# A four-layer convolution network: layer 2's patches stored as lines by column offsets by channels, and the product instructions that read them

## The chip, the core and the metric

The kernel runs on one core of a Trainium2 chip. The metric is the device time of one execution in microseconds (us); the median of the runs of the kernel before is 8996.71 us. The engines are named as the profile names them: PE (TensorE) multiplies matrices, PEld loads its weights, DVE is VectorE, ACT is ScalarE, POOL is GpSimd, and SP is the queue from which this kernel issues its DMAs. SBUF is the on-chip memory of 128 partitions; PSUM is the memory that TensorE writes.

## The reference: what is computed

The input is 16 images of 64 x 64 positions with 256 channels, all float32. Four layers follow one another, each of the form `x = x + layer(groupnorm(x))`. The change concerns layer 2 alone, an involution: a small network makes nine weights for each position and each of 16 groups of channels, and these weigh the 3 x 3 patch of a projected image.

```
r = relu(norm(x @ Wr + br))                         # 64 channels
w = (r @ Ws + bs).reshape(B, H, W, G, KK)[:, :, :, :, None, :]
xi = x @ Wi + bi
xp = pad(xi)                                        # one position on each side
patches = stack([xp[:, i:i+H, j:j+W, :] for i in range(3) for j in range(3)], axis=3)
patches = patches.reshape(B, H, W, G, F // G, KK)
out = sum(w * patches, axis=-1)                     # 256 channels
```

The reshape is what makes the order of numbers matter. Before it, a position's 2304 numbers are ordered by tap (three lines by three columns) and then by channel. After it, the same 2304 numbers are cut in order into 256 outputs of nine numbers each. So output channel o takes the numbers 9 o to 9 o + 8 of the run. These nine are nine neighbouring channels of one tap, or, where the run passes from one tap to the next, the last channels of one and the first ones of the other. Sixteen neighbouring outputs share a group, and so the nine weights.

## The kernel before

**Stages.** The kernel runs through four stages with pools of their own: layer 0 and the gates of layer 1, then layer 1's scan, then a stage in which the end of layer 1, all of layer 2 and the preparation of layer 3 overlap, and at last layer 3. Only the third stage holds the change. In the profile its products run from 3865 to 6521 us.

**Turns.** The third stage is a loop over turns with an order of instructions written out by hand (`tc.manual_schedule()`). Each image has NCH = 8 turns, and a turn takes four lines of the upper half of an image together with four lines of the lower half; a column position and a half make up the 128 partitions (`(w g)`, w the 64 columns, g the half). Four jobs run in each turn, each for another image, offset by `LAG = (0, 12, 20, 30)` turns: the end of layer 1 (`end_of_layer1`), the projection Wi (`projected`), the involution, and the centring of the finished output for layer 3 (`centred`). A job drops out where its images have ended, so that the involution runs in 128 turns, the first 10 of them without centring and the last 20 or so without the end of layer 1.

**What a turn issues, in order.**
- SP: the loads for the next turn (`loads`, L964: x2p and x2r, which are layer 2's input for the projection and for the weights; x1 and pf for the end of layer 1), the stores of the turn before (L1241: x2, x3, c3, and 16 `strips` stores for centred lines), then the load of xc for the next turn's centring. xc has two buffers, so its load waits until the strips of two turns before have been read. x2p has two buffers too, so its load waits for the projection (L1061) that read the older one.
- TensorE: the later half's weights (`weights`, L1092); the preparation of the next turn, which is the reduction Wr (`reduced2`, L1082), the patches' transposes (L1108) and the first half's weights; the residual's transposes (`residual`, L1128, tile lo); the finished turn's transposes (`turned`, L1162); the projection (L1061).
- ScalarE: the preparation's activation (L1085) and the patch copies out of PSUM (L1112) with the copies at the seams (L1114, L1118), all in `patches`; then the activation on z (L1004) of the end of layer 1, the copies of the finished turn (L1163), the projection's activation into the padded lines (L1065), and squares for the statistics (L1183, L1015).
- GpSimd: two additions of the end of layer 1 (L1008), which need ScalarE's z; then the sums of the first half (`sums_on_pool`: three additions L1149 and one L1150), then the subtraction of the mean in `centred` (L900).
- VectorE: two instructions of the end of layer 1 (L998, tiles z and pf), the products of the first half and of the second half (`products`, L1138), the sum of the second half over nine (a reduction, L1284), and two additions of the residual (L1287), the second of which needs GpSimd's L1150.

When the next turn is the first of an image, its preparation is put behind the first half's products, because the padded lines are only complete then. The norms between the layers are chains of small instructions that are advanced one piece at each `step()`.

**Patches.** `patches` makes for each turn three tiles xs, one for each column offset j (pool `b_xs`, six buffers). A tile holds six lines (four and one more on each side) of 256 channels, and eight more numbers at the end of each line. These eight are the first channels of the next offset (L1114) or, behind the third offset, those of the next line (L1118), so that nine numbers that pass a seam can be read from one tile.

**Products.** `involution_segments` cuts the 256 outputs wherever a tap begins and wherever a group of 16 begins. That gives 24 segments, each with its tap, its first channel, its first output and its count n. For each segment one instruction multiplies four lines by n outputs by nine numbers with the group's nine weights, which lie in PSUM (pw) and are read again for each of the n outputs. The result goes to the tile pd, [128, 4, 128, 9] for a half of 128 outputs. Twelve segments belong to each half. Eight segments of the 24 have all 16 outputs of a group, 576 numbers in each partition; the others have 36 to 540. Together they are 9216 numbers in each partition and turn.

Of the kernel before, what the change touches and what calls it, by code (L numbers as in the profile page):

```python
# [9 lines left out]
F32 = mybir.dt.float32  # L10
# [5 lines left out]
P = 128  # L16
C = 256
# [13 lines left out]
TILE_IN = (TR + 6) * (TC + 6)  # L31
TILE_OUT = TR * TC
SPAN = P + (TR - 1) * (TC + 6) + TC - 1


def involution_segments():

    cuts = sorted({-(-tap * C // 9) for tap in range(10)} | set(range(0, C + 1, 16)))  # L40
    return [(9 * o // C, 9 * o % C, o, n - o) for o, n in zip(cuts, cuts[1:])]


@with_exitstack
def network(ctx: ExitStack, tc: tile.TileContext, a: dict, out: bass.AP):
    nc = tc.nc
# [138 lines left out]
    with ExitStack() as st:  # L185
# [399 lines left out]
        for n in range(LAST + 16):  # L585
            m, t = divmod(n, NCH)
# [26 lines left out]
            def between(dp):  # L613
                step()
                if dp == 0:
                    for p in parts:
                        if p is not parts[0]:
                            next(p)
                    for p in parts:
                        next(p, None)  # L620
                    for p in old:
                        next(p, None)
                    for p in projecting:
                        next(p)
# [26 lines left out]
    with ExitStack() as st:  # L651
# [24 lines left out]
        with tc.tile_pool(name="s_conv", bufs=1) as pcv:  # L676
# [20 lines left out]
            for delta in range(-2, 3):  # L697
                for rr in range(2):
                    for r2 in range(2):
                        di = 2 * delta + rr - r2 + 3  # L700
# [8 lines left out]
        for n in range(10):  # L709
            delta, c = n // 2, n % 2  # L710
# [28 lines left out]
        with tc.manual_schedule():  # L739
# [25 lines left out]
            for n, (ch, g) in enumerate(steps):  # L765
# [18 lines left out]
                b, k = g * 8, min(8, NI - g * 8)  # L784
# [8 lines left out]
        n = NI * NCH  # L793
        pt = tr.tile([P, CT], F32, tag="tr", name="pt")
# [125 lines left out]
    with ExitStack() as st:  # L920
        pc = st.enter_context(tc.tile_pool(name="b_const", bufs=1))
        wk = st.enter_context(tc.tile_pool(name="b_work", bufs=2))
        xs_p = st.enter_context(tc.tile_pool(name="b_xs", bufs=6))
        pd_p = st.enter_context(tc.tile_pool(name="b_pd", bufs=2))
        tr = st.enter_context(tc.tile_pool(name="b_tr", bufs=3, space=PSUM))
        pwp = st.enter_context(tc.tile_pool(name="b_pw", bufs=3, space=PSUM))
# [23 lines left out]
        for b in range(2):  # L950
# [2 lines left out]
            nc.vector.memset(rt[64:65, :], 1.0)  # L953
            rts.append(rt)

        segments = involution_segments()
        st0, st3, gn2, ngm2 = {}, {}, {}, {}
        loaded, stores, begun = [], [], []

# [138 lines left out]
        def patches(i, rc, between):  # L1098


            xs = []
            for j in range(3):
                t = xs_p.tile([P, 6, C + 8], F32, tag="xs", name="xs")
                for e in range(0, 6, 2):
                    pt = tr.tile([P, 2, C], F32, tag="tr", name="pt")
                    for k in range(2):
                        for h in range(2):
                            nc.tensor.transpose(  # L1108
                                pt[:, k, h * P : (h + 1) * P],
                                lines[:, h, rc * 4 + e + k, 2 * j : 2 * j + P], ident,  # L1110
                            )
                    nc.scalar.copy(t[:, e : e + 2, 0:C], pt)  # L1112
                if j:
                    nc.scalar.copy(xs[-1][:, :, C:], t[:, :, 0:8])  # L1114
                xs.append(t)
                if j == 0:
                    between()
            nc.scalar.copy(xs[2][:, 0:5, C:], xs[0][:, 1:6, 0:8])  # L1118
            return xs

        def residual(x2):
# [8 lines left out]

        def products(oh, pw, xs):
            pd = pd_p.tile([P, 4, P, 9], F32, tag="pd", name="pd")
            for tap, c0, o, n in segments:
                if o // P != oh:
                    continue
                di, dj = tap // 3, tap % 3
                w0 = o // 16 * 9 - oh * 72
                nc.vector.tensor_tensor(  # L1138
                    pd[:, :, o - oh * P : o - oh * P + n, :],
                    xs[dj][:, di : di + 4, c0 : c0 + 9 * n].rearrange("p r (f k) -> p r f k", k=9),  # L1140
                    pw[:, :, w0 : w0 + 9].unsqueeze(2).broadcast_to([P, 4, n, 9]),
                    ALU.mult,
                )
            return pd
# [87 lines left out]
        with tc.manual_schedule():  # L1232
            loads(0)
            ahead, made = None, None
            for n in range(TURNS):
# [21 lines left out]
                def prepare():  # L1257
                    x2r, rt = reduced2(*nxt)
                    ahead = [x2r, rt]
                    ahead.append(patches(*nxt, lambda: ahead.append(weights(rt, 0))))  # L1260
                    return ahead
# [11 lines left out]
                if inv:  # L1273
                    pd = products(0, now[2], now[3])
                    sums_on_pool(pd, x3)
                if nxt and not nxt[1]:
                    ahead = prepare()
                if inv:
                    pd1 = products(1, w1, now[3])
# [19 lines left out]
    with ExitStack() as st:  # L1299
# [201 lines left out]
        for n, (i, quarter, t) in enumerate(turns):  # L1501
# [45 lines left out]
            if n in features:  # L1547
                tp, k = features[n]
# [118 lines left out]
```

## Time and profile before

| what | value |
|---|---|
| runs shown | 8993.86, 8996.71, 9007.82 us |
| span of the profiled execution, first to last instruction | 8940.3 us |
| median less span, what lies around it | 56.4 us |
| mean granted TensorE clock | 0.913 |
| stretch 4112 to 5249 us (1137 us): VectorE busy | 1080 us |
| the same stretch: TensorE, ScalarE, GpSimd busy | 858, 714, 802 us |
| the same stretch: DMA engines busy, bytes moved | 0.82, 223 GB/s |
| the same stretch: granted TensorE clock | 0.85 |

No time is listed beside the profiled execution but its span, so what lies around that span is taken from the median of the runs. In the page's list of costliest groups a line reads: source line, engine, operation, output and inputs by name with partitions x elements, the count, then after the first bar the busy time of the group in us and the mean of one instruction in ns, and after the second bar the idle time of the engine just before these instructions and what ended most of it. Busy time counts a moment once even where two instructions of an engine overlap, so it can be less than count by mean. In the list of waits a line reads: engine and line that waited, what it waited for, the total in us, how often, and the longest. In the timeline a line reads: start and length in us, engine, line, operation and operands, the number of instructions merged, and in brackets the idle time before it with what ended it; SPq is the issuing of DMAs. In the slices each digit stands for 223.5 us.

### The profile page before, as it was taken

To read this page: it belongs to the slowest core of one execution; us is meant where nothing else is said; L and a number is where in the kernel's file an instruction comes from. 1 tells how busy PE (TensorE), PEld (TensorE's weight loads), DVE (VectorE), ACT (ScalarE), POOL (GpSimd) and SP (SyncE) were. 2 spreads that over 40 slices of the span, in tenths; PEclk is the share of its full clock that TensorE was granted. 3 is DMA by queue.
4 is the path that set the end of the run, shared out by engine and by line. 5 is a ranking of instruction groups with operands and counts; after the bars stand their busy time and mean duration, and the time that the engine had idled before them with its cause. 6 is when DMAs were issued, how large, how long until landed. Compare 5 with 4: busy or idle time off the path is not lost. (4 is left out here: it accounts for less than half of the span.)

```text
span 8940.3 us, 213550 instructions
## 1 busy us (share of the span) xinstructions
PE 7239.3 (81%) x84764; PEld 5334.1 (60%) x84764; DVE 6515.6 (73%) x10687; ACT 5059.9 (57%) x12288; POOL 2767.6 (31%) x1962
## 2 busy tenths in 40 slices
PE   7988889888899977477777777777758888888888
PEld 4666666666666653145545444455546666777776
DVE  6676666676666665679999999999945555566665
ACT  3555555555555554666666666665535555566665
POOL 0111111111111110156776776776621111111122
PEclk9999999999999986888888888888879999999999
DMA  6533333333333333767888888887768787888887
GB/s 220 167 121 123 125 123 122 124 123 120 125 109 105 108 110 110 257 205 209 220 225 225 221 227 220 221 230 208 186 165 256 243 252 240 254 258 260 267 260 244
DMA packets 1617992, 1695.63 MB, mean 190 GB/s; under 512 B 855265, under 2 KB 1221170, under 8 KB 1615842
## 3 DMA queue, kind: packets, MB, share of 16 engines
q1 hardware_dynamic: 1616994, 1681.98, 62.1%
q8 instruction: 668, 10.94, 0.5%
q14 instruction: 330, 2.70, 0.1%
HBM read 1234.54 MB, written 469.76 MB: 191 GB/s over the span
## 5 line engine op out<-in xcount | busy, mean ns | idle before, releaser
L287 PE MATMUL pq<-wq,xn 128*128 128x384 f32 x4096 | 1471.9, 503 | 105.3 <-DVE va L303 57.5
L1138 DVE TENSOR_TENSOR pd<-xs,pw 128x576 f32<-128x576 f32 (+15 forms) x3072 | 1438.2, 554 | 10.0 <-PE pw L1092 6.6
L1403 ACT ACTIVATE wm<-pk,spanb 128x176 f32<-128x176 f32 x2560 | 988.6, 543 | 520.8 <-PE pk L1393 500.4
L1408 DVE TENSOR_TENSOR wm<-pk,spanb 128x704 f32<-128x704 f32 x896 | 1174.5, 1354 | 142.5 <-PE pk L1393 130.2
L1393 PE MATMUL pk<-rt,span 64*128 64x176 f32 x12288 | 1199.2, 331 | 96.3 <-issue 44.3
L1149 POOL TENSOR_TENSOR pd<-pd 128x2048 f32<-128x2048 f32 (+2 forms) x384 | 1065.4, 2775 | 296.3 <-DVE pd L1138 276.3
L287 PEld LDWEIGHTS pq<-wq,xn 128*128 128x128 f32 x4096 | 762.7, 195 | 573.8 <-DVE va L303 90.9
L1393 PEld LDWEIGHTS pk<-rt,span 64*128 64x128 f32 x12288 | 982.0, 193 | 196.6 <-issue 67.7
L1477 POOL TENSOR_TENSOR ex<-ex,rx 128x192 f32<-128x192 f32 (+2 forms) x768 | 435.4, 570 | 1855.5 <-DVE ex L1470 1211.0
L1459 PE MATMUL pa<-wm,xw 126*32 126x48 f32 x45056 | 701.4, 211 | 237.2 <-issue 198.3
L1470 DVE SCALAR_TENSOR_TENSOR ex<-pa,msk,ex 128x192 f32<-128x192 f32 x704 | 292.1, 415 | 745.9 <-ACT ex L1469 717.5
L1459 PEld LDWEIGHTS pa<-wm,xw 126*32 126x32 f32 x45056 | 578.1, 112 | 410.7 <-issue 341.1
L1061 PE MATMUL px<-x2p,wis 128*128 128x512 f32 x1024 | 581.4, 711 | 139.6 <-ACT c L1163 99.5
L1108 PEld LDWEIGHTS pt<-ident,pad 128*128 128x128 f32 x4608 | 542.1, 151 | 252.5 <-issue 78.0
L1108 PE MATMUL pt<-ident,pad 128*128 128x128 f32 x4608 | 628.2, 292 | 74.4 <-ACT rt L1085 43.3
L1112 ACT COPY xs<-pt 128x512 f32<-128x512 f32 x1152 | 604.1, 588 | 139.6 <-PE pt L1108 137.4
L456 POOL TENSOR_TENSOR rsy<-ss,mhalf 128x4 f32<-128x4 f32 x128 | 129.8, 1014 | 1704.2 <-DVE ss L454 1704.2
L1284 DVE TENSOR_REDUCE x<-pd 128x512 f32<-128x4608 f32 x128 | 634.1, 4954 | 1.9
L444 PE MATMUL py<-wo,oT 128*128 128x256 f32 x2048 | 472.5, 383 | 28.9 <-DVE va L303 28.9
L1469 ACT ACTIVATE ex<-pa,msk 128x192 f32<-128x192 f32 x704 | 297.6, 423 | 330.7 <-PE pa L1459 229.2
L1082 PE MATMUL pr<-x2r,wrs 128*64 128x512 f32 x512 | 317.7, 754 | 198.3 <-DMA x2r<-x_d 185.2
L303 DVE COPY va<-pq 128x256 f32<-128x256 f32 x512 | 216.6, 423 | 336.2 <-ACT ka L299 315.3
(240 smaller groups left out, 12764.3 us busy)
## 6 DMA issues: line engine op xcount, KB each, us to landing
xw<-strips SPq DMA_DIRECT2D x1408, 256.0 KB
xn<-in_x SPq DMA_DIRECT2D x256, 512.0 KB
x_d<-x SPq DMA_DIRECT2D x256, 512.0 KB
strips<-xc SPq DMA_DIRECT2D x1536, 56.0 KB
xin<-in_x SPq DMA_DIRECT2D x128, 512.0 KB
x<-in_x SPq DMA_DIRECT2D x128, 512.0 KB
xm<-x_d SPq DMA_DIRECT2D x128, 512.0 KB
x<-x_d SPq DMA_DIRECT2D x128, 512.0 KB
```

The lines of the kernel that those rows point to most:

```text
L287: nc.tensor.matmul(pq[:, dd, 0:384], lhsT=xn[:, h, tok], rhs=wq[:, h, hf * 384 : (hf + 1) * 384], start=(h == 0), stop=(h == 1),)
L444: nc.tensor.matmul(py[:, q, :], lhsT=oT[hf][:, q * P : (q + 1) * P], rhs=wo[:, hf, :], start=(hf == 0), stop=(hf == 1),)
L1061: nc.tensor.matmul(px, lhsT=w[:, h, fh * P : (fh + 1) * P], rhs=x2[:, h], start=(h == 0), stop=(h == 1),)
L1108: nc.tensor.transpose(pt[:, k, h * P : (h + 1) * P], lines[:, h, rc * 4 + e + k, 2 * j : 2 * j + P], ident,)
L1112: nc.scalar.copy(t[:, e : e + 2, 0:C], pt)
L1138: nc.vector.tensor_tensor(pd[:, :, o - oh * P : o - oh * P + n, :], xs[dj][:, di : di + 4, c0 : c0 + 9 * n].rearrange("p r (f k) -> p r f ...
L1149: nc.gpsimd.tensor_tensor(pd[..., 0:n], pd[..., 0:n], pd[..., n : 2 * n], ALU.add)
L1284: nc.vector.tensor_reduce(x3[:, :, P:C], pd1, AX.X, ALU.add)
L1393: nc.tensor.matmul(pkv[:, b, m], lhsT=span[half, first + gg, s0 : s0 + P], rhs=rto[half, o // 4 * 2 + m, :], start=True, stop=True,)
L1403: nc.scalar.activation(dst[:, m // 2, m % 2], pkv[:, m // 2, m % 2], AF.Identity, bias=spanb[:, g0 + m : g0 + m + 1],)
L1408: nc.vector.tensor_tensor(dst, pkv, spanb[:, g0 : g0 + 4].rearrange("p (b m) -> p b m", b=2).unsqueeze(3).broadcast_to([P, 2, 2, NTL]), AL ...
L1459: nc.tensor.matmul(pav[p0 : p0 + 32, :, tj * TC : (tj + 1) * TC], lhsT=xw[0:TILE_IN, k, tj, 32 * q : 32 * q + 32], rhs=wm[q][0:TILE_IN, (t ...
```

## The change

The three tiles of a turn become one block, six lines by three column offsets by 256 channels, with two buffers. In it a line's three offsets lie one behind the other, and the next line follows at once; so the 2304 numbers of an output line (three lines by three offsets by 256 channels) are one run in memory. The eight extra numbers per line and the copies at the seams (L1114 and L1118 before) go, and `involution_segments` goes with them. The products are cut by line and half: an instruction takes one of four output lines and one half, 1152 numbers of the run as eight groups by 16 outputs by nine numbers, with the line's weights in PSUM read for each of the 16 outputs. That is 8 instructions a turn, where there were 24. The tile pd, the sums, the transposes and the nine patch copies (two lines of 256 channels each) keep their shapes; a patch copy now writes its two lines 768 numbers apart and not 264.

```diff
-def involution_segments():
-    cuts = sorted({-(-tap * C // 9) for tap in range(10)} | set(range(0, C + 1, 16)))
-    return [(9 * o // C, 9 * o % C, o, n - o) for o, n in zip(cuts, cuts[1:])]
...
-        xs_p = st.enter_context(tc.tile_pool(name="b_xs", bufs=6))
+        xs_p = st.enter_context(tc.tile_pool(name="b_xs", bufs=2))
...
-            xs = []
+            xs = xs_p.tile([P, 6, 3, C], F32, tag="xs", name="xs")
             for j in range(3):
-                t = xs_p.tile([P, 6, C + 8], F32, tag="xs", name="xs")
                 for e in range(0, 6, 2):
...
-                    nc.scalar.copy(t[:, e : e + 2, 0:C], pt)
-                if j:
-                    nc.scalar.copy(xs[-1][:, :, C:], t[:, :, 0:8])
-                xs.append(t)
+                    nc.scalar.copy(xs[:, e : e + 2, j, :], pt)
                 if j == 0:
                     between()
-            nc.scalar.copy(xs[2][:, 0:5, C:], xs[0][:, 1:6, 0:8])
             return xs
...
             pd = pd_p.tile([P, 4, P, 9], F32, tag="pd", name="pd")
-            for tap, c0, o, n in segments:
-                if o // P != oh:
-                    continue
-                di, dj = tap // 3, tap % 3
-                w0 = o // 16 * 9 - oh * 72
+            for r in range(4):
+                run = xs[:, r : r + 3].rearrange("p e j c -> p (e j c)")
                 nc.vector.tensor_tensor(
-                    pd[:, :, o - oh * P : o - oh * P + n, :],
-                    xs[dj][:, di : di + 4, c0 : c0 + 9 * n].rearrange("p r (f k) -> p r f k", k=9),
-                    pw[:, :, w0 : w0 + 9].unsqueeze(2).broadcast_to([P, 4, n, 9]),
+                    pd[:, r].rearrange("p (g f) k -> p g f k", f=16),
+                    run[:, oh * 9 * P : (oh + 1) * 9 * P].rearrange(
+                        "p (g f k) -> p g f k", f=16, k=9
+                    ),
+                    pw[:, r].rearrange("p (g k) -> p g k", k=9).unsqueeze(2).broadcast_to(
+                        [P, 8, 16, 9]
+                    ),
                     ALU.mult,
                 )
             return pd
```

More of the change, by code (lines that the diff above doesn't have):

```diff
@@ L954, in network @@
             rts.append(rt)
-        segments = involution_segments()
         st0, st3, gn2, ngm2 = {}, {}, {}, {}
```

## The prediction

> **What bounds the kernel now.** The products run in one stage, layer 2, from 3865 to 6521 us. I read first the page's slices and costliest groups, to see which engine is full there.
>
> ```profile
> DVE  6676666676666665679999999999945555566665
> ...
> POOL 0111111111111110156776776776621111111122
> ...
> DMA  6533333333333333767888888887768787888887
> ...
> L1138 DVE TENSOR_TENSOR pd<-xs,pw 128x576 f32<-128x576 f32 (+15 forms) x3072 | 1438.2, 554 | 10.0 <-PE pw L1092 6.6
> ...
> L1284 DVE TENSOR_REDUCE x<-pd 128x512 f32<-128x4608 f32 x128 | 634.1, 4954 | 1.9
> ```
>
> VectorE is at nine tenths and the products are more than half of it, but the DMA engines are at eight tenths and move only 223 GB/s. A full engine need not set the pace, so I read who the DMA queue (SP) waits for, first in 3850 to 4100 us, then in 5200 to 6130 us, then in 6530 to 6600 us:
>
> ```profile
> SPq L964 <- PE px L1061: 146.5, 12, 17.3
> ```
> ```profile
> SPq L964 <- DMA strips<-xc: 78.7, 90, 2.1
> ...
> SPq L964 <- PE px L1061: 3.7, 8, 0.7
> ```
> ```profile
> SPq L1309 <- PE pv L156: 15.5, 1, 15.5
> ```
>
> At first SP waits for compute in each turn (a load needs the buffer that projected, L1061, has not yet read). In the middle it waits for nothing but DMAs. At the very end it waits 15.5 us for compute, before the first load of layer 3. Now the timeline: the loads of x2r mark SP's turns, the products VectorE's.
>
> ```profile
> 5331.19 0.43 SPq L964 DMA_DIRECT2D x2r<-x_d  x1
> ...
> 5353.83 0.43 SPq L964 DMA_DIRECT2D x2r<-x_d  x1
> ...
> 5375.68 0.43 SPq L964 DMA_DIRECT2D x2r<-x_d  x1
> ```
> ```profile
> 5343.67 11.23 DVE L1138 TENSOR_TENSOR pd<-xs,pw 128x576 f32<-128x576 f32 x24
> 5354.94 4.95 DVE L1284 TENSOR_REDUCE x<-pd 128x512 f32<-128x4608 f32 x1
> 5360.00 1.34 DVE L1287 TENSOR_TENSOR x<-x,lo 128x512 f32<-128x512 f32 x2
> 5361.83 1.64 DVE L998 SCALAR_TENSOR_TENSOR z<-x,ngm,pf 128x512 f32<-128x512 f32 x1 [0.49 <-DMA pf<-fac_d]
> 5363.51 0.75 DVE L998 SCALAR_TENSOR_TENSOR pf<-x,ngm,pf 128x512 f32<-128x512 f32 x1
> ```
>
> I listed all 128 x2r loads and reductions (number i: the i-th of each) and took differences:
> - Head, i = 0 to 12 (to 4112 us): reductions 18.9 to 20 us apart, but for i = 1 (25.9) and two turns after an image's end (24.5 and 22.6). VectorE sets the pace.
> - Middle, to i = 108 (6175 us): SP's turns stay at 20.6 to 22.6 us, mean 21.58 from i = 9 to 65 and 21.6 from 65 to 105. VectorE needs 20.0 to 20.5, and 25 to 30 once per image. It starts behind and closes up: reduction i comes 69.7 us after load i at i = 9, 47.5 at 65, then never under 42.6. From there it takes SP's pace, and TensorE waits for SP:
>
> ```profile
> PE pr L1082 <- DMA x2r<-x_d: 115.6, 28, 7.8
> ```
> - Tail, i = 108 to 127: layer 1's loads have ended. SP's turn is 18.0, VectorE's 17.5 and without a gap (11.23 products, 4.95 reduction, 1.28 additions). VectorE sets the pace.
>
> [...] Trace: 24 products of 9216 elements take 11.23 us, so (11.23 - 9.60 - 0.09)/24 = 64 ns each, the 0.09 being the last one's own tail[...]. [...] z (L998) takes 0.75 us alone, and 1.64 above while GpSimd's subtraction runs (L900, to 5362.92); products always take 11.23 for 24. [...]
>
> **The change part by part.** Groups by form in 4500 to 6500 us:
>
> ```profile
> L1138 DVE TENSOR_TENSOR pd<-xs,pw 128x576 f32<-128x576 f32 x768 | 578.6, 753 | 4.9 <-PE pw L1092 4.9
> ...
> L1138 DVE TENSOR_TENSOR pd<-xs,pw 128x288 f32<-128x288 f32 x192 | 78.9, 457 | 0.0
> ...
> L1114 ACT COPY xs<-xs 128x48 f32<-128x48 f32 x192 | 44.5, 232 | 6.1
> ...
> L1118 ACT COPY xs<-xs 128x40 f32<-128x40 f32 x96 | 21.1, 220 | 0.0
> L1138 DVE TENSOR_TENSOR pd<-xs,pw 128x36 f32<-128x36 f32 x96 | 18.5, 192 | 0.0
> ```
>
> 1. Products. From 36 to 576 elements the time grows 561 ns for 540, 1.04 ns each[...]. So 8 instructions of 1152 need 8 x 1.20 + 8 x 0.064 + 0.09 = 10.20 us, not 11.23: 1.03 less a turn, half in each half. One should show 1152/0.96 + 154 = 1.35 us (154 is what 753 has over 576/0.96). Inner runs stay 9 long; outer steps change, and no row has this form. Bounds: all fixed cost gone, -1.54 us; a tenth slower streaming, back to nothing. I take 1.03.
> 2. The copies at seams: 2 x 232 + 220 = 0.68 us of ScalarE a turn. They lie ahead of z's activation (L1004), GpSimd's additions (L1008) and its sums (L1149) in ScalarE's and GpSimd's order. Hidden by VectorE in most turns of head and tail; on the path after an image's end, where VectorE waits 4.45 us at 4048 us for the sums, two preparations being in that chain (1.37 us).
> 3. Patch copies (L1112) stay nine of 512 elements, 588 ns, with a longer step between two lines: taken at nothing, as VectorE's turn covers it; +-20 ns each would be +-0.18 us where ScalarE isn't covered.
> 4. Buffers: one block per turn twice, not three tiles six times, equally two turns deep. A block is free when the later half's last product is done, a turn before it is written: nothing (were that order to fail, a patch copy would wait for products, up to 10.2 us). The products' waits, for pw and for the copies, are those of before, and no DMA, matrix or GpSimd instruction moves: their order is unchanged.
> 5. New wait? GpSimd's sums and last addition take 8.45 + 1.65 = 10.1 us from the end of the first products; VectorE reaches its addition after 5.1 + 4.98 + 0.65 = 10.7 (11.2 before). 0.6 us to spare, so none of its own.
>
> Where it counts:
> - Head: i = 0 about 0.7 (half of products, or copies), 1 to 6 six full turns 6.2, the image's end 1.4, i = 9 1.0, then 0.5 each for two turns in which z now stands longer before GpSimd's subtraction. 10 us, handed to SP, which waits there for compute.
> - Middle: SP's turn of 21.6 stays. VectorE (about 19.2) only catches up sooner. Once locked, the way from x2r's landing to the reduction loses 0.68 + 1.03, a single gain of about 2.
> - Tail: 19 turns x 1.03 = 19.6, less about 0.6 at the image's end: 19.
> Sum 31. Against it: x2r lands about 7.5 us after issue (TensorE waits for it at 6395.87 for 6388.37), then 3.6 projection, 0.8, 7 patches, 10.2 products = 29 us least lag; the last lag of 48.4 would fall to 27, so 2 come back. And SP's 15.5 us rest before layer 3, in which its transfers drain, goes: about 3. SP itself ends 10 earlier, plus 5 that it waits for GpSimd's subtractions (L900) in the tail, so it can follow. Result 31 - 2 - 3 = 26 us.
>
> The profiled span is 8940.3 us, the median of the runs 8996.7; the 56 between lie outside the span. I take 26 off both: 8914 and 8971.
>
> **The rivals.**
> - A: SP sets the pace of the tail too (its turn of 18.0 is over VectorE's 17.5 already, with few waits for compute). Then only the head counts: 10 us, 8987. For it: 24 transfers a turn, 16 of them strips of 10.5 us in all. Against: the lag grows from 37.9 to 48.4 in the tail, and the 15.5 us wait at its end. Chance 0.20.
> - B: VectorE sets the pace throughout, and SP only looks free: 128 x 1.03 = 132 us, 8865. For: 0.95 busy. Against: VectorE closing up on SP by 22 us in the middle. Chance 0.07.
> - C, slower: [...] From 10.7% slower on (1.03 of 9.6) the turn grows. At 25% it is 2.40 - 1.03 = 1.37 more a turn, over 10 + 19 turns of head and tail 40; in the middle 20.3 + 1.4 is just over SP's 21.6, and the 25 to 30 once per image is no longer made up, some 5 for each of 12 images, 60 more: 9097. For: untried pattern. Against: 36 to 576 elements on one line. Chance 0.07.
> - D: it doesn't do what it says, the fixed cost being tied to something other than the count: 8997, chance 0.05.
>
> **How the numbers follow.** The forecast has 0.61, with its own range 8961 to 8982. A measurement of this kernel can tell about 0.2%, 18 us: faster means under 8979, slower over 9015. The forecast gives 0.53 faster and 0.08 same, A 0.20 same, B 0.07 faster, D 0.05 same, C 0.07 slower; that is 0.60, 0.33 and 0.07. The range takes in A: 8955 to 8993; B, C and most of D lie outside, under 0.2.
>
> **What would show it.** Products near 1.35 us each and 10.2 for 8; no seam copies; SP's turns 21.6 in the middle as before; first strips issued about 10 us earlier; reductions 16.5 apart in the tail; the lag falling sooner and ending near 29; the wait ahead of layer 3's first load mostly gone. It is wrong if the middle's turns shorten (B), if the tail's reductions stay 17.5 or TensorE waits for x2r in each of its turns (A), or if a product takes over 1.5 us (C).

## The result and the profile after

The kernel after takes 8967.52 us (median of five runs, 8952.84 to 8976.86), the kernel before 8996.71 us (8991.18 to 9008.92) on the same chip. That is 29 us less, a ratio of 0.9963 with a 95% interval of 0.9951 to 0.9975.

The execution profiled after has a span of 8974.9 us and took 8976.86 us. So 2 us lie around a span, not the 56 that stood between the first profile and its median. Two further profiles of the kernel before show the same 2 us: spans of 8937.8 and 8949.0 us for times of 8939.59 and 8950.74. The first profile, with a span of 8940.3 us, therefore belongs to an execution of about 8942 us, some 50 us faster than every run listed beside it. That it came from another chip is an estimate, from the 8946.59 us that the kernel before takes on the chip of e1 to e4; the record does not show it. So the spans of the two first profiles are not subtracted from one another, and the time is followed piece by piece on one chip below. Lengths of instructions and kinds of waits are still read side by side.

From the page of the kernel after, three slices and VectorE's two rows of the involution:

```profile
DVE  6676666776666665679989988999946565566665
...
POOL 0111111111111110157766666676712121111112
...
DMA  6533333333333333867878878887768888888887
...
L1121 DVE TENSOR_TENSOR pd<-xs,pw 128x1152 f32<-128x1152 f32 x1024 | 1305.6, 1349 | 13.3 <-ACT xs L1102 13.3
...
L1271 DVE TENSOR_REDUCE x<-pd 128x512 f32<-128x4608 f32 x128 | 633.7, 4951 | 1.9
```

VectorE has lost some of its nines in the middle, while the DMA digits stay. The products cost 133 us less (1438.2 before), while the run is 29 us shorter. The waits of SP, in the windows of the prediction (3850 to 4100, 5200 to 6130, and the last stretch before layer 3, 6480 to 6600 us):

```profile
SPq L955 <- PE px L1052: 132.4, 13, 15.7
```
```profile
SPq L955 <- DMA strips<-xc: 79.2, 94, 2.5
...
SPq L955 <- PE px L1052: 8.2, 13, 1.1
```
```profile
SPq L1296 <- PE pv L148: 2.1, 1, 2.1
```

SP waits less for compute in the head (132.4 us for 146.5), still for hardly anything but DMAs in the middle, and 2.1 us instead of 15.5 ahead of layer 3's first load. SP's timeline and VectorE's in the middle:

```profile
5344.20 0.43 SPq L955 DMA_DIRECT2D x2r<-x_d  x1
...
5366.03 0.43 SPq L955 DMA_DIRECT2D x2r<-x_d  x1
...
5387.13 0.43 SPq L955 DMA_DIRECT2D x2r<-x_d  x1
```
```profile
5355.91 10.20 DVE L1121 TENSOR_TENSOR pd<-xs,pw 128x1152 f32<-128x1152 f32 x8
5366.14 4.95 DVE L1271 TENSOR_REDUCE x<-pd 128x512 f32<-128x4608 f32 x1
5371.20 0.69 DVE L1274 TENSOR_TENSOR x<-x,lo 128x512 f32<-128x512 f32 x1
5373.01 0.69 DVE L1274 TENSOR_TENSOR x<-x,lo 128x512 f32<-128x512 f32 x1 [1.12 <-POOL x L1137]
5374.23 1.61 DVE L989 SCALAR_TENSOR_TENSOR z<-x,ngm,pf 128x512 f32<-128x512 f32 x1 [0.53 <-DMA pf<-fac_d]
```

SP's turns are 21.8 and 21.1 us, as long as before. The products have fallen to 10.20 us, and VectorE now waits between its two additions and ahead of z. TensorE's wait for x2r in 5200 to 6130 us was 122.1 us before and is now

```profile
PE pr L1073 <- DMA x2r<-x_d: 163.5, 31, 8.3
```

Much of what VectorE saves in the middle (1.03 us in each of this window's 43 turns, 44 us) returns as waiting for SP's loads (41 us more). Groups by form, 4500 to 6500 us:

```profile
L1121 DVE TENSOR_TENSOR pd<-xs,pw 128x1152 f32<-128x1152 f32 x768 | 979.2, 1349 | 9.4 <-ACT xs L1102 9.4
...
L1102 ACT COPY xs<-pt 128x512 f32<-128x512 f32 x864 | 444.0, 602 | 92.4 <-PE pt L1098 90.2 <-DVE z L989 0.3 <-DVE pd L1121 0.2
```

The seam copies are gone; a patch copy is recorded with 602 ns, where it had 588.

### The profile page after: what moved, and what is told of

It reads as the page before. It is cut to its first block, busy times and chain, and to the rows that moved or that the text cites. A ratio compares the mean times of both kernels' runs of the same rounds, so it can differ in the third digit from the quotient of the medians.

```text
span 8974.9 us, 210876 instructions
## 1 busy us (share of the span) xinstructions
PE 7219.9 (80%) x84764; PEld 5328.9 (59%) x84764; DVE 6420.8 (72%) x8639; ACT 4992.0 (56%) x11904; POOL 2764.1 (31%) x1962
## 5 line engine op out<-in xcount | busy, mean ns | idle before, releaser
L1121 DVE TENSOR_TENSOR pd<-xs,pw 128x1152 f32<-128x1152 f32 x1024 | 1305.6, 1349 | 13.3 <-ACT xs L1102 13.3
L1380 PE MATMUL pk<-rt,span 64*128 64x176 f32 x12288 | 1217.4, 334 | 108.5 <-issue 58.5
L1073 PE MATMUL pr<-x2r,wrs 128*64 128x512 f32 x512 | 364.5, 853 | 374.3 <-DMA x2r<-x_d 368.5
L1052 PE MATMUL px<-x2p,wis 128*128 128x512 f32 x1024 | 531.7, 664 | 111.4 <-ACT c L1150 68.2
L445 ACT ACTIVATE sq<-y 128x256 f32<-128x256 f32 x512 | 213.0, 416 | 422.6 <-DVE y L441 414.6
```

The lines of the kernel that those rows point to most:

```text
L1052: nc.tensor.matmul(px, lhsT=w[:, h, fh * P : (fh + 1) * P], rhs=x2[:, h], start=(h == 0), stop=(h == 1),)
L1121: nc.vector.tensor_tensor(pd[:, r].rearrange("p (g f) k -> p g f k", f=16), run[:, oh * 9 * P : (oh + 1) * 9 * P].rearrange("p (g f k) -> ...
L1380: nc.tensor.matmul(pkv[:, b, m], lhsT=span[half, first + gg, s0 : s0 + P], rhs=rto[half, o // 4 * 2 + m, :], start=True, stop=True,)
```

## The experiments

The theory is the prediction's: SP sets the pace in the middle, VectorE in head and tail. The rivals are A (SP in the tail too) and B (VectorE throughout). Each run is compared with the kernel before on its own chip: 8946.59 us for e1 to e4, 8985.80 for e5 to e8, 8956.67 for e9 to e12. "Stage" is the time from the first reduction of layer 2 to the first product of layer 3 in the profile (tile pk); it leaves out what an execution happens to lose elsewhere. The expectations were written with the first chip's 8996.71 us in mind, so what counts in them is the distance to the kernel before or after.

| run | time, us | ratio to before, interval | stage, us |
|---|---|---|---|
| e1 before | 8939.59 (single run) | | 2730.4 |
| e2 after, third xc buffer | 8829.66 | 0.9874 (0.9861 to 0.9888) | 2617.5 |
| e3 before, third xc buffer | 8916.83 | 0.9970 (0.9958 to 0.9981) | 2688.4 |
| e4 after, 32 products in the middle | 8918.63 | 0.9972 (0.9963 to 0.9982) | 2704.1 |
| e5 after | 8942.21 | 0.9952 (0.9938 to 0.9966) | 2716.2 |
| e6 after, 64 products in the head | 8972.64 | 0.9988 (0.9981 to 0.9994) | 2749.0 |
| e7 after, 64 products in the tail | 9007.94 | 1.0029 (1.0018 to 1.0039) | 2785.1 |
| e8 after, one more load a turn | 9057.47 | 1.0083 (1.0069 to 1.0097) | 2838.2 |
| e9 before | 8950.74 (single run) | | 2734.8 |
| e10 after | 8927.70 (single run) | | 2709.7 |
| e11 e2 with seam copies | 8898.94 | 0.9932 (0.9920 to 0.9944) | 2686.8 |
| e12 e2 with a late subtraction | 8988.90 | 1.0032 (1.0020 to 1.0045) | 2769.4 |

**e1, e5, e9, e10: the two kernels again**, without an edit.

> The kernel before, unchanged, profiled a second time, to set the two profiles side by side from the same day's chip. The first profile of before spans 8940 us while its runs take 8991 to 9009; the profile of after spans 8975 while its runs take 8953 to 8977. Theory (SP sets the pace in the middle of layer 2, and the rest is chance of the execution): the products' stage, from the first reduction to the last, takes 2643 us as in the first profile (within 8), and layer 3 takes anything between 2328 and 2375. Rival (the change itself made layer 3 some 40 us longer): layer 3 takes 2328 again, within 5.

> After, unchanged, timed beside before on one chip, so that the edits can be set against it. On the chip of the first experiments before took 8946.6. Both theories: 29 us under before, within 8; profile: products' stage from first to last reduction 14 us shorter than in before, as in the first profile of after, or 25 if the middle's slower SP turns there were chance of that execution.

> Before, unchanged, profiled beside after on the same chip, since the profiles so far came from chips of different speed. Theory (SP's turn in the middle is the chip's, not the form's): from load 14 to load 105 both take the same within 5 us; from the first reduction to the first load of layer 3, after is 20 to 28 us shorter; layer 3 is equal within 8. Rival (the faster form itself lengthens SP's turn, by 0.1 us a turn): the middle is 8 us or more longer in after.

> After, unchanged, profiled beside before on the same chip; the numbers are those said for before.

On the second chip the change is worth 44 us, which is 7 more than e5's expectation allowed (29 within 8); its interval, 31 to 56 us, overlaps that of the first chip, 22 to 44. The single runs on the third differ by 23. e1 does not decide its question: layer 3 takes 2331.6 us, which the theory (2328 to 2375) and the rival (within 5 of 2328) both allow. The profiles of e9 and e10 decide it, and let the time be followed piece by piece (the i-th x2r load and the i-th reduction of 128, counted from 0, as in the prediction):

| piece | e9 before | e10 after | difference |
|---|---|---|---|
| first instruction to first reduction | 3878.2 | 3882.5 | +4.3 |
| head: first reduction to x2r load 14 | 228.0 | 214.2 | -13.8 |
| middle: x2r load 14 to 108 | 2027.6 | 2026.2 | -1.4 |
| lag: load 108 to reduction 108 | 43.6 | 41.3 | -2.3 |
| tail: reduction 108 to 127 | 344.7 | 337.1 | -7.6 |
| last reduction to first product of layer 3 | 90.9 | 90.9 | 0.0 |
| layer 3 | 2336.0 | 2333.5 | -2.5 |

The stage is 25 us shorter. SP's turn in the middle is 21.57 us before and 21.56 after, and layer 3 differs by 2.5 us, so both rivals fall: the new form lengthens neither.

**e4: the middle's products in 32 instructions of 288 numbers.** Turns 30 to 99 only; k is the number of the turn, and g0 runs over the eight groups of a line and half.

```diff
+            m = 2 if 30 <= k < 100 else 8
...
-                nc.vector.tensor_tensor(
-                    pd[:, r].rearrange("p (g f) k -> p g f k", f=16),
...
+                for g0 in range(0, 8, m):
+                    o = (oh * 8 + g0) * 144
+                    nc.vector.tensor_tensor(
+                        pd[:, r, g0 * 16 : (g0 + m) * 16].rearrange("p (g f) k -> p g f k", f=16),
...
```

> After, with the products of the middle alone (turns 30 to 99 of the 128) cut into 32 instructions of 288 numbers, not 8 of 1152: 24 x 0.064 = 1.54 us more VectorE a turn. SP theory: VectorE's turn of 19.2 becomes 20.7, still under SP's 21.7, so nothing but slack goes: 8968 to 8985. Rival VectorE: 70 x 1.54 = 108 more, 9075.

It is 28 us faster than the kernel before (12 to 29 were expected), within the 23 to 44 of the kernel after, though its middle's turns hold 24 instructions more. The first of the two waits, 4550 to 6140 us, is of e4, the second of the kernel after:

```profile
PE pr L1073 <- DMA x2r<-x_d: 234.7, 51, 7.1
```
```profile
PE pr L1073 <- DMA x2r<-x_d: 281.9, 54, 8.7
```

Of the 108 us that the products add (70 turns by 1.54), 47 are seen here as less waiting of TensorE for x2r (in the same window e9, the kernel before, has 159.2 us and e10, the kernel after, 277.1); the rest was not followed. SP's turn is 21.54 us, 21.52 in e1 on the same chip. Rival B, by which this kernel had to be some 80 us slower than the kernel before, falls.

**e6: the head's products in 64 instructions of 144 numbers**, e4's edit with `m = 1 if 0 <= k < 12 else 8`.

> After, with the products of the first 12 turns alone cut into 64 instructions of 144 numbers: 56 x 0.064 = 3.6 us more VectorE in each of these turns. SP theory: in the head SP waits for compute, so 12 x 3.6 = 43 us are handed to it and are never made up: 35 to 45 us over after. Rival (slack of the middle absorbs a late head, as the distance between SP and VectorE falls from 60 to 43 anyway): under 20 us over after.

It takes 30 us more than e5. The timeline of e6 shows a turn of the head:

```profile
3919.97 4.95 DVE L1272 TENSOR_REDUCE x<-pd 128x512 f32<-128x4608 f32 x1
3925.03 1.28 DVE L1275 TENSOR_TENSOR x<-x,lo 128x512 f32<-128x512 f32 x2
3926.24 0.74 DVE L989 SCALAR_TENSOR_TENSOR z<-x,ngm,pf 128x512 f32<-128x512 f32 x1
3927.02 0.75 DVE L989 SCALAR_TENSOR_TENSOR pf<-x,ngm,pf 128x512 f32<-128x512 f32 x1
3927.68 13.81 DVE L1124 TENSOR_TENSOR pd<-xs,pw 128x144 f32<-128x144 f32 x64
```

The products take 13.81 us, 3.61 more than 10.20, and VectorE has no gap. x2r load 14 leaves 243.2 us after the first reduction, 213.7 in e5. These 29.5 us stay to the end: the head hands what it loses to SP, and the rival (under 20) falls. The forecast of 35 to 45 was too high, since not every turn loses 3.6 us: from one reduction to the next turns 2 to 8 lose 3.6, but turn 1 only 0.7 and turn 9, at the image's end, 0.9, and turn 12 gains 1.0 back.

**e7: the tail's products in 64 instructions**, e4's edit with `m = 1 if 108 <= k < 128 else 8`.

> After, with the products of the last 20 turns alone cut into 64 instructions: 3.6 us more VectorE in each, a turn of 20.1 against SP's 18.0. Theory (VectorE sets the pace of the tail and the entry into layer 3 waits for it): 20 x 3.6 = 72, less the slack of SP's end, which is at most a few us: 60 to 72 us over after. Rival A (SP sets the pace of the tail too): only what exceeds SP's 18.0, 20 x 2.1 = 42 or less.

It takes 66 us more than e5. Of 20 turns by 3.61 = 72, nine tenths arrive. The wait of SP ahead of layer 3 is back:

```profile
SPq L1297 <- PE pv L148: 19.3, 1, 19.3
```

SP is done and waits, so VectorE is what the tail ends with. Rival A falls.

**e8: one more load a turn.** In turns 35 to 124 x2p is loaded a second time, into a tile that nothing reads. To have room, two tiles of layer 0 and 1 (`maps`, `fac`) move to a pool that is closed ahead of the stage; e2, e3, e11 and e12 do so too.

```diff
+            if proj and 35 <= n < 125:
+                t = wk.tile([P, 2, CT], F32, tag="x2q", name="x2q", bufs=1)
+                nc.sync.dma_start(out=t, in_=x2_d[proj[0], proj[1]])
```

> After, with one more load of 512 KB a turn (x2p a second time into a tile that nobody reads) in 90 turns of the middle, no work for any engine changed. SP theory: at 223 GB/s, 512 KB are 2.3 us of SP's turn, so 90 x (1.5 to 2.3) = 135 to 210 us over after. Rival VectorE: nothing, within 10.

It takes 115 us more than e5, 1.28 us for each of 90 loads; SP's turn goes from 21.63 to 22.90 us. The price, 135 to 210, was put too high, but a transfer that gives no engine any work goes into the time, where B had nothing. TensorE's wait for x2r, 4550 to 6140 us, in e8:

```profile
PE pr L1076 <- DMA x2r<-x_d: 358.9, 58, 11.9
```

**e2 and e3: a third xc buffer**, after and before. The strips and the load behind them no longer wait for the strips of two turns ago.

```diff
-            ))
+            ), bufs=3)
```

> After, with a third buffer for xc, so that its load need not wait for the strips of two turns before to land (4 KB more for each partition, found by giving two tiles that are dead by then a pool of their own). SP theory: SP waits 1.9 us a turn for this in the middle (138 us in 155 waits from 4550 to 6140 us); its turn falls from 21.7 to about 19.8, VectorE's own turn (19.2, and once per image more, 20.2 in the mean) then decides, and 94 turns x 1.4 = 130 us go: 8835, from 8800 to 8900. Rival VectorE (it sets the pace already): within 10 of 8968. Rival DMA throughput (the engines, not the queue's order, are full): the wait comes back as longer issues, SP's turn stays above 21.2, 8930 to 8968.

> Before, with the same third buffer for xc. SP theory: VectorE's own pace in the middle is 21.2 in the mean, SP's 21.6, so 95 x 0.4 = 38 us go: 8958, from 8930 to 8975; and the product change is then worth 8958 - 8835 = 120 us, four times what it is worth with two buffers. Rival VectorE: 8997, and the difference between the two forms stays at 29. Rival DMA throughput: 8960 to 8997, difference still about 29.

With SP's wait gone, e3 is 30 us faster than the kernel before and e2 117: where SP no longer sets the pace, the change is worth 87 us instead of 23 to 44. SP's turn in the middle falls to 20.59 us in e2 (21.52 in e1), with the same transfers, so the rival that the DMA engines themselves are full falls too. SP's waits in e2, 4300 to 6000 us, show that it now waits for compute, the DMA that headed the list being gone from its top:

```profile
SPq L958 <- PE px L1055: 69.9, 19, 6.4
SPq L1231 <- POOL xc L894: 57.2, 31, 4.8
SPq L1231 <- DMA x_d<-x: 56.8, 118, 2.1
```

This is the fastest kernel, 1.26% under the kernel before. But 87 is not the 120 expected, and z is why in part: its mean in this window is 1476 ns in e2 and 1202 in e3. In the first profiles of the two kernels (3860 to 6180 us) a z that meets no subtraction of GpSimd's takes 0.74 to 0.76 us (64 and 69 of them), and each one that meets one (L900 before, L892 after) ends 0.54 to 0.62 us behind it (44 and 40), whether it began early or late in it. So a VectorE that comes sooner makes z longer. A second part is one turn of each image, three after the one that follows an image's end: from one reduction to the next it takes 22.6 us in e2 and 20.5 in e3 (mean of turns 30 to 104).

**e11: e2 with the seam copies alone put back.** They write a tile that nothing reads.

```diff
+            seam = wk.tile([P, 6, 8], F32, tag="seam", name="seam", bufs=2)
...
+                if j:
+                    nc.scalar.copy(seam, xs[:, :, j, 0:8])
...
+            nc.scalar.copy(seam[:, 0:5, :], xs[:, 1:6, 0, 0:8])
```

> After with the third buffer for xc, and with the three copies at the seams put back on ScalarE (into a tile that nobody reads), the products as in after. This splits the 87 us that the change is worth with the third buffer (8916.8 to 8829.7 on one chip) into its two parts. Theory (the copies only count in the chain after an image's end, two preparations each): 15 images x 1.4 = 21 us over the third buffer alone, so 96 us under before instead of 117. Rival (the copies lie ahead of GpSimd's sums in each turn): 60 us or more of the 87. Rival (all is the count of instructions): within 5.

Of the 117 us against the kernel before 58 are left, so the copies cost 59 of the change's 87; by the stages (own chip's before taken off) it is 65 of 71. The 21 us expected were far too few, and the rival that only the count of instructions matters falls. The other rival has nearly the right size (60 or more), but not the place, as it had the copies count in each turn. The wait of VectorE for GpSimd's sums and of GpSimd for z's activation, 4300 to 6000 us, in e2 and then in e11:

```profile
DVE x L1277 <- POOL x L1140: 66.8, 20, 5.5
```
```profile
POOL x L1002 <- ACT z L998: 208.0, 62, 10.0
```
```profile
DVE x L1281 <- POOL x L1144: 121.5, 20, 9.1
```
```profile
POOL x L1002 <- ACT z L998: 314.2, 60, 13.6
```

As many turns, 20, wait nearly twice as long in all. Mean turns by place in the image (turns 30 to 104) tell where (from one reduction to the next): e2 has 24.7 us in the turn after an image's end and 22.6 three turns later, e11 29.1 and 24.0; the other six differ by 0.1 at most. 5.8 us an image hang on copies of 0.68 us, two preparations of which (1.37) lie in that chain. Why it is four times their own length was not found. That it lies in the chain ScalarE, GpSimd, VectorE is shown by the two waits.

e11 set against e3 leaves the count of instructions, 8 for 24, since both have copies at the seams and the third buffer (e11's copies write another tile, and the chips differ). It is worth 28 us by the times and only 6 by the stages. In the middle it brings nothing: x2r load 14 to 108 takes 1996.0 us in e11 and 1980.1 in e3, and the two chips differ there by only 5 (2027.6 and 2022.9 for the kernel before). Six turns of each image are about 0.5 us shorter, but the two in which VectorE waits for GpSimd's sums are longer, 29.1 and 24.0 us for 27.5 and 20.5.

**e12: the subtraction of the centring a turn later**, with a fourth xc buffer, so that z should be free of it.

```diff
+                if late:
+                    centred(*late)
                 if inv:
...
-                if cen:
-                    centred(*cen)
+                late = cen
```

> After with a fourth buffer for xc and GpSimd's subtraction of the mean (2.37 us) moved from the end of a turn into the next turn, behind the two additions and ahead of the sums, where GpSimd waits 2.4 us for products anyway. With the third buffer alone z on VectorE takes 1.46 us in the mean, not 0.75[...]; theory: VectorE's turn loses 0.7 to 1.2 us in some 90 turns, but SP's issues alone are near 19 us a turn, so 40 us (20 to 70) are gained over the third buffer alone: 137 to 187 us under before. Rival (SP and the DMA engines now decide): within 15 of the third buffer alone, 102 to 132 under before.

The time went the other way: it is 32 us slower than the kernel before. z did what was hoped, the sums did not, 4300 to 6000 us of e12:

```profile
L992 DVE SCALAR_TENSOR_TENSOR z<-x,ngm,pf 128x512 f32<-128x512 f32 x77 | 57.6, 748 | 1.6 <-ACT sq L1173 0.4
```
```profile
DVE x L1279 <- POOL x L1140: 240.9, 37, 10.3
```

On GpSimd the additions, the moved subtraction and the sums stand in this order, and where z comes late from ScalarE all of them are late. One such turn, GpSimd first and then VectorE:

```profile
5006.62 2.36 POOL L894 TENSOR_TENSOR xc<-xc,gmb 128x1024 f32<-128x1024 f32 x1
5008.94 8.49 POOL L1139 TENSOR_TENSOR pd<-pd 128x2048 f32<-128x2048 f32 x3
...
5019.22 0.69 DVE L1279 TENSOR_TENSOR x<-x,lo 128x512 f32<-128x512 f32 x1 [7.26 <-POOL x L1140]
```

The moved subtraction, 2.36 us ahead of the sums, is only a part of these 7.26 us: ScalarE's last piece of z had only ended at 5004.8 us, after ScalarE had waited 12.02 us for the projection. Such waits of ScalarE come to 481.4 us in this window, 313.6 in e2; why they grew was not followed.

## Why the prediction was right, step by step

- **Products.** One took 1349 ns for 1350 forecast, eight 10.20 us for 10.20. The rate behind the forecast (1.04 ns an element, so 9.60 us for 9216, or 0.96 elements per ns) is that of the profile before, 540 elements in 561 ns. It holds in the new form: 1152 elements took 596 ns more than 576 (753), 1.03 ns each. The fixed cost follows the count, with 9216 elements a turn each time: from 8 to 24 instructions (11.23 - 10.20)/16 = 64 ns each, from 8 to 64 (13.81 us, e6) (13.81 - 10.20)/56 = 64 ns. C (more time for each element) and D (a fixed cost that doesn't follow the count) fall with it.
- **Middle.** Right: nothing. SP's turn did not move with the products' count (21.57 and 21.56; 21.54 in e4) but moved with one more load (22.90). The time shifts into TensorE's wait for x2r (122.1 and 163.5 us, above).
- **Head.** Forecast 10 us; the first strips come 10.5 us sooner after the first reduction in the first pair of profiles (212.0, 201.5), 13.4 in e9 and e10 (214.9, 201.5). Right: ordinary turns there went from 19.0 to 17.9 us, near the products' 1.03, and 3 of the 13.4 are one turn of e9, the one at the image's end, which took 27.5 us there and 24.5 in both other profiles of the kernel before.
- **Lag once locked.** Forecast 2, measured 2.3.
- **Tail.** Forecast 19, less 2 for x2r's supply, so 17; measured 7.6 in e9 and e10. This term was mis-sized, though not by a fixed amount: the first pair has 9.5 (346.3, 336.8), and e4, whose tail is that of the kernel after, is 13.7 under e1 on the same chip (332.7, 346.4). Ordinary turns did shrink as said; reductions in e10 are 16.5 us apart where e9 has 17.5. But the three turns around the image's end at i = 112 stayed at 23.1, 19.0 and 18.8 (22.8, 18.9 and 18.9), and those after the next one grew to 20.1 and 21.9 (17.5 and 18.8). There the floor that the prediction named was met, the lag falling to 28.4 us in e10 and 29.2 in the first profile of the kernel after (29 forecast; at the very end it is 31.8 and 32.8), but these two turns cost some 6 us in e10, not 2. VectorE's timeline in e10, 6365 to 6425 us:

```profile
6368.89 10.20 DVE L1121 TENSOR_TENSOR pd<-xs,pw 128x1152 f32<-128x1152 f32 x8 [3.51 <-ACT xs L1102]
...
6386.25 10.20 DVE L1121 TENSOR_TENSOR pd<-xs,pw 128x1152 f32<-128x1152 f32 x8
6400.93 0.16 DVE L137 COPY gm<-pg 128x2 f32<-128x2 f32 x1 [4.48 <-PE pg L131]
```

  First the patches are late; here the profile names no wait for x2r but one of ScalarE for a store (c_d, 3.57 us), ahead of the projection. Then a norm's small copy (L137) holds VectorE 4.48 us ahead of its reduction: TensorE has the norm's product (L131) behind the next turn's preparation, which had waited 8.81 us for x2r. In 6170 to 6525 us TensorE waits 55.9 us for x2r in 13 waits, in e9 23.1 in 8, so rival A's sign shows in part of the tail.
- **SP's rest of 15.5 us.** It went, as forecast (2.1), but the 3 us that this was to cost did not come: from the last reduction to layer 3's first product it is 90.9 us before and after. Together with the head's 4 more, most of which is that one turn of e9, and 1.4 in the middle this covers for the tail. The step is right, but that 25 us of stage stand so near the 26 forecast is in part luck.
- **Seam copies.** Taken at 1.4 us an image in the head and else as hidden. With two xc buffers nothing contradicts it, but no run took the copies apart from the products there. With three, where SP does not set the pace, they are the larger part of the change, 5.8 us an image (e11); the step had priced their own length and not what queues behind them.
- **Patch copies.** Taken at nothing. They are recorded 14 ns longer, but not for the longer step: e11 has the new block and 588 ns. Between seam copies they are recorded shorter (588 ns, in the kernel before too, for 602); why was not followed.
- **The 56 us around the span.** Wrong, as said above: 2. It did no harm, since the same number was taken off both.

Two things stay open. With two xc buffers no run separates the copies' part of the gain from the products'. And the size of the gain, 23 to 44 us, is not known more closely; since the intervals of the two chips overlap, it isn't shown that it depends on the chip.

The first reduction comes later in the three profiles of the kernel after (3882.5 to 3886.8 us from the start, 3875.8 to 3878.2 before). This goes with the execution and not with the change: e5 and e6, both of the new form and on one chip, have 3883.7 and 3873.3, and e4 has 3876.6 where e1 on its chip has 3875.8.

## What to carry to other kernels

An engine that is 95% busy need not set the pace: VectorE was (1080 of 1137 us before), and 1.03 us less work a turn left the middle's turn where it was (21.57 and 21.56 us). List the start of each turn on the queue and on the engine, and see which of the two keeps its rhythm when the other has room. Fewer, larger instructions saved 64 ns each on VectorE, exactly as counted, but the saving reached the end only where that engine was the slower one and did not run into another engine's wait: of e9's and e10's 25 us the head has 13.8 and the tail 7.6, the middle 1.4. Here a third buffer for one tile, which frees the queue, raised what the whole change was worth from under 45 to 87 us, and most of that (59) was due to three short copies, not to the count of instructions. These were priced by what waits in line behind them on two other engines, 5.8 us an image, not by their own length there, 1.37.

## What the hardware showed unexpectedly

The kernel before has medians of 8946.59, 8956.67, 8985.80 and 8996.71 us on the chips of these runs, 0.56% apart; the change is 0.37%. A profile of one chip beside times of another misleads by more than what is measured.

z, the same instruction with the same operands, took 0.74 us in e6's head, where no centring runs yet, 1.2 to 1.5 us on average in the middle (1202 ns in e3, 1476 in e2), and up to 2.91 us in the kernel after (at 5461.59 us), with GpSimd's subtraction running from 5461.58 to 5463.95 us. So part of any time saved ahead of it is given back there, 0.27 us a turn between e3 and e2.
